# Layer 2 of a graph network: edge weights as 16-bit exponent bits, three bf16 parts of the support, and an order by hand

## The chip, the cores and the metric

The kernel runs on one core of a Trainium2 chip. The metric is the device time of one execution in microseconds (us), as the median of several executions.

Engines are named as the profile names them: PE (TensorE, matmuls), PEld (its weight loads), DVE (VectorE), ACT (ScalarE), POOL (GpSimd) and SP (which issues most transfers). PSUM is the memory in which PE leaves its sums. A record is one instruction in the profile; "issue" in a chain of waits is time in which an engine waited for nothing that the profile shows. The granted clock (PEclk) is the share of its full clock that PE ran at.

## The reference

Four graph layers act on 3327 nodes with 64 features and a dense 3327 x 3327 adjacency matrix, each as `x = x + layer(relu(layernorm(x)), adj)`. Only layer 2 is edited:

```python
def layer2(input, adj, weight, bias):
    support = input @ weight
    mask = (adj != 0).astype(support.dtype)
    rank = jnp.cumsum(mask, axis=1)
    deg = rank[:, -1:]
    k = jnp.minimum(deg, 100.0)
    pos = rank - (deg - k)
    w = mask * jnp.where(pos > 0, 0.5 ** (k - pos), 0.0)
    return w @ support + bias
```

So an edge weighs 0.5 to the power of the number of edges behind it in its row, and nothing where that is 100 or more.

## The kernel before

The nodes are 26 blocks of 128. The targets (3328 with padding) are two halves of 1664, each four quarters of 416 columns (`CH`). An accumulator bank `acc[q]` holds both halves of the aggregation: the first on PSUM partitions 0 to 63, the second on 64 to 127, because there are only 64 features. Layers 0 and 1 use the same helper.

```python
def accumulate(acc, q, h, lhsT, rhs, first, last):
    T.matmul(acc[q][h * D : (h + 1) * D, :CH], lhsT=lhsT, rhs=rhs, start=first, stop=last)
```

Layer 2 goes through the source blocks from the last. `tri` is a strict triangle with -1024 on its diagonal, `behind` the sum of the masks of all blocks already done. One number per edge slot therefore holds both the count and whether there is an edge. The weight is made of the exponent bits of a float32. In what follows, a count is a matmul with `tri` or `ones`, an accumulation one into `acc`, and a change of kind the step of PE from one to the other.

```python
for j in reversed(range(NB)):
    a = adj_block(j)                       # 128 sources x 3328 targets, f32, 3 buffers
    V.tensor_scalar(mask, a, 0.0, None, op0=OP.not_equal)
    for h in range(2):
        for q in range(NQ):
            i0 = h * HN + q * CH
            p = scratch("cnt")
            T.matmul(p[:, :CH], lhsT=tri, rhs=mask[:, i0 : i0 + CH], ...)
            if behind is not None:
                T.matmul(p[:, :CH], lhsT=ones, rhs=behind[:, i0 : i0 + CH], ...)
            S.activation(bits, p[:, :CH], AF.Relu, bias=ebias, scale=-EXP_UNIT)   # int32
            V.scalar_tensor_tensor(w, p[:, :CH], MAX_NEIGH - MASK_ON, bits.bitcast(F32),
                                   op0=OP.is_lt, op1=OP.mult)
            pending.append((q, h, m_n[:, slot(j), :], w, j == NB - 1, j == 0))
            flush(2)                       # accumulates all but the last two
    ...
    V.tensor_add(nxt, behind, mask)        # the running sum, for the next block
```

A scheduler orders the instructions of layers 0 to 2. Layer 3, the longest, is ordered by hand in both kernels.

## Time and profile before

| | before |
|---|---|
| median of the runs | 1997.71 us (1993.67 to 1998.79) |
| busy in the profiled execution (1998.0 us) | PE 68%, DVE 68%, ACT 34%, POOL 21% |
| layer 2, first count to last accumulation | 465.2 to 749.7: 284.5 us |
| one source block in it | 11.06 us |

In layer 2 the two steps from count to weight are these groups of the page. A row gives the line, engine and operation, what it writes from what and how often; then its busy time and the mean of one in ns; then the idle time of the engine ahead of it and who ended most of that.

```profile
L392 ACT ACTIVATE bits<-cnt,ebias 128x416 int32<-128x416 f32 x208 | 123.3, 607 | 167.9 <-PE cnt L384 156.0
L394 DVE SCALAR_TENSOR_TENSOR w<-cnt,bits 128x416 f32<-128x416 f32 x208 | 115.6, 586 | 50.9 <-ACT bits L392 50.7
```

They are hops from engine to engine: ACT idles mostly for the counts, DVE for ACT. Idle time of ACT here costs nothing by itself.

### The profile page before, as it was taken

The page shows a single profiled execution, that of the slowest core. Times are in us where ns is not written, and L with a number is a line of the kernel's source. Part 1 is how long each engine was busy: PE and PEld are TensorE (multiplying, and loading weights), DVE is VectorE, ACT ScalarE, POOL GpSimd, SP SyncE. Part 2 cuts the span into 40 slices and gives each one's busy share as a digit, 9 for nine tenths or more (in the row PEclk, how much of TensorE's full clock was granted, in tenths as well). Part 3 has the DMA queues.
Part 4 walks back from the last instruction along what each step waited for, and adds up shares of the span by engine and source line. Part 5 has one row for each costly group of instructions (what it writes and reads, how often), then busy time and mean ns, then how long its engine had stood idle before and what let it go on. Part 6 is the DMA issues. An engine that isn't in the chain of part 4 may idle for free.

```text
span 1998.0 us, 10423 instructions
## 1 busy us (share of the span) xinstructions
PE 1358.2 (68%) x3689; PEld 563.7 (28%) x3689; DVE 1349.5 (68%) x1269; ACT 686.8 (34%) x613; POOL 421.4 (21%) x118
## 2 busy tenths in 40 slices
PE   5999968937999992666566656646566656656640
PEld 3344333313222222222223322223223322222310
DVE  2021062067777768788888788886888788888878
ACT  0010011013444440454444445442644445444440
POOL 0000000000000000334433333440533333443330
PEclk9999988978999995666666566657665666666565
DMA  7985934961444101111111111110211111111000
GB/s 294 398 326 216 390 147 177 394 249 69 153 155 156 50 0 53 34 34 36 63 39 34 35 34 34 41 62 0 65 37 34 35 34 35 41 61 34 17 0 17
DMA packets 24373, 204.01 MB, mean 102 GB/s; under 512 B 5505, under 2 KB 5633, under 8 KB 12545
## 3 DMA queue, kind: packets, MB, share of 16 engines
q1 hardware_dynamic: 21312, 202.84, 27.1%
q10 hardware_dynamic: 3008, 0.50, 0.1%
q8 instruction: 29, 0.48, 0.1%
q14 instruction: 24, 0.19, 0.0%
HBM read 202.48 MB, written 0.85 MB: 102 GB/s over the span
## 4 chain that ended last, share of the span: by engine, by line
issue 34%; PE 27%; POOL 16%; DVE 14%; DMA 7%; ACT 1%; ACTq 0%; POOLq 0%; DVEq 0%
PE acc L233 17%; POOL lnp L567 9%; POOL sig L560 7%; DMA adj<-in_adjT 7%; DVE behind L408 2%; PE cnt L376 2%; PE cnt L384 2%; PE pd L532 1%; PE pd L535 1%; DVE sq L73 1%; PE ac L575 1%; PE pd L493 1%; DVE dist L554 1%; DVE w L394 1%; DVE den L540 1%
## 5 line engine op out<-in xcount | busy, mean ns | idle before, releaser
L532 PE MATMUL pd<-auge,augj 66*128 66x416 f32 x416 | 288.9, 791 | 237.7 <-DVE den L533 237.7
L560 POOL TENSOR_TENSOR sig<-sig,adj 128x1664 f32<-128x1664 f32 x52 | 213.1, 4117 | 1099.7 <-ACT sig L559 1099.7
L575 PE MATMUL ac<-lnp,hn 128*65 128x416 f32 x416 | 210.6, 674 | 190.2 <-DVE lnp L572 183.8
L535 PE MATMUL pd<-augd,augj 66*128 66x416 f32 x416 | 284.5, 781 | 0.0
L233 PE MATMUL acc<-adj,m_n 128*64 128x416 f32 x1056 | 270.2, 518 | 13.7 <-DMA adj<-in_adjT 13.6
L567 POOL TENSOR_TENSOR lnp<-lnp,dist 128x1664 f32<-128x1664 f32 x52 | 205.6, 3956 | 135.2 <-ACT dist L566 135.2
L544 ACT ACTIVATE den<-den 128x1664 f32<-128x1664 f32 x52 | 82.7, 1590 | 426.9 <-DVE den L540 388.5
L554 DVE TENSOR_SCALAR dist<-dist 128x1664 f32<-128x1664 f32 x52 | 222.3, 4275 | 1.8
L532 PEld LDWEIGHTS pd<-auge,augj 66*128 66x128 f32 x416 | 116.6, 288 | 361.3 <-DVE den L533 255.7
L249 DVE COPY m_t<-acc 128x416 f32<-128x416 f32 x12 | 6.3, 584 | 305.9 <-PE acc L233 305.9
L233 PE MATMUL acc<-w,m_n 128*64 128x416 f32 x416 | 184.0, 534 | 18.7 <-DVE w L394 18.7
L537 DVE SCALAR_TENSOR_TENSOR dist<-den,pd 128x416 f32<-128x416 f32 x208 | 122.4, 588 | 104.6 <-PE pd L535 95.4
L551 DVE SCALAR_TENSOR_TENSOR dist<-dist,den 128x1664 f32<-128x1664 f32 x52 | 182.0, 3501 | 9.1 <-ACT den L547 9.1
L392 ACT ACTIVATE bits<-cnt,ebias 128x416 int32<-128x416 f32 x208 | 123.3, 607 | 167.9 <-PE cnt L384 156.0
L533 DVE TENSOR_SCALAR den<-pd 128x416 f32<-128x416 f32 x208 | 122.2, 588 | 68.7 <-PE pd L532 68.3
L575 PEld LDWEIGHTS ac<-lnp,hn 128*65 128x65 f32 x416 | 72.0, 181 | 340.3 <-DVE lnp L572 216.4
L233 PEld LDWEIGHTS acc<-adj,m_n 128*64 128x64 f32 x1056 | 112.5, 136 | 168.0 <-issue 131.9
L535 PEld LDWEIGHTS pd<-augd,augj 66*128 66x128 f32 x416 | 120.8, 291 | 123.5 <-issue 103.4
L394 DVE SCALAR_TENSOR_TENSOR w<-cnt,bits 128x416 f32<-128x416 f32 x208 | 115.6, 586 | 50.9 <-ACT bits L392 50.7
L565 ACT ACTIVATE lnp<-dist,one 128x1664 f32<-128x1664 f32 x52 | 87.4, 1681 | 128.2 <-DVE dist L554 127.9
L571 DVE TENSOR_TENSOR lnp<-lnp,den 128x1664 f32<-128x1664 f32 x52 | 98.0, 1885 | 7.2 <-POOL lnp L567 7.2
L572 DVE TENSOR_TENSOR lnp<-lnp,sig 128x1664 f32<-128x1664 f32 x52 | 98.4, 1892 | 1.8
(200 smaller groups left out, 1233.0 us busy)
## 6 DMA issues: line engine op xcount, KB each, us to landing
adj<-in_adjT SPq DMA_DIRECT2D x88, 1664.0 KB, 8.4
adj<-in_adjT SPq DMA_DIRECT2D x52, 832.0 KB, 4.5
res<-in_adjT SPq DMA_DIRECT2D x4, 1664.0 KB, 8.3
xn<-in_x SPq DMA_DIRECT2D x1, 832.0 KB, 5.0
out<-u SPq DMA_DIRECT2D x1, 832.0 KB, 3.4
ih<-in_wihT ACTq DMA_DIRECT2D x4, 48.0 KB, 4.8
hh<-in_whhT ACTq DMA_DIRECT2D x4, 48.0 KB, 9.8
w<-in_W ACTq DMA_DIRECT2D x4, 16.0 KB, 5.5
```

The source lines that it names most:

```text
L233: T.matmul(acc[q][h * D : (h + 1) * D, :CH], lhsT=lhsT, rhs=rhs, start=first, stop=last)
L392: S.activation(bits, p[:, :CH], AF.Relu, bias=ebias, scale=-EXP_UNIT)
L394: V.scalar_tensor_tensor(w, p[:, :CH], MAX_NEIGH - MASK_ON, bits.bitcast(F32), op0=OP.is_lt, op1=OP.mult,)
L532: T.matmul(p[:, :CH], lhsT=lhsT, rhs=auge[:, cs], start=True, stop=True)
L533: V.tensor_scalar(e[:, cs], p[:, :CH], MIN_NORM, None, op0=OP.max)
L535: T.matmul(p[:, :CH], lhsT=lhsT, rhs=augd[:, cs], start=True, stop=True)
L537: V.scalar_tensor_tensor(d[:, cs], e[:, cs], 2e-7, p[:, :CH], op0=OP.mult, op1=OP.max)
L551: V.scalar_tensor_tensor(dist[j], dist[j], LN_SCALE**0.5, den[j], op0=OP.mult, op1=OP.mult)
L554: V.tensor_scalar(dist[j], dist[j], ONE_LESS, None, op0=OP.min)
L560: G.tensor_mul(s, s, adjs.pop((hf, j)))
L567: G.tensor_sub(l, l, dist[j])
L575: T.matmul(acc[q][: D + 1, :CH], lhsT=hn[:, slot(j), :], rhs=l[:, q * CH : (q + 1) * CH], start=j == 0, stop=j == NB - 1,)
```

## The change

The intent: take the product off DVE by letting ACT alone make the weight. With the bias changed to `(100 - 1024) * 2**7`, the ReLU gives `(100 - count) * 128` for an edge and zero otherwise. As a 16-bit integer these are the bits of a bf16 power of two, scaled by 2**-27. The support is scaled by 2**27 and cut into three bf16 parts whose sum is exact, so that all matmuls of the loop are bf16. Counts now come in tiles of two banks. A half block is one pass of the loop over `k`: two quarters of both target halves, with 8 counts and 12 accumulations. Its accumulations stand together, with the target halves alternating, and the order of the instructions is that of the text (`manual_schedule`). The rest of the diff gives up the four scratch banks of PSUM for the loop and takes them back after it (so that the two-bank count tiles fit), and removes comments.

```diff
-EXP_UNIT = 2.0**23
+EXP_UNIT = 2.0**7
...
             linear(h_t, w_l2, m_n)
+            V.tensor_scalar(m_n, m_n, 2.0**27, None, op0=OP.mult)
+            parts = []
+            for i in range(3):
+                p = mk.tile([P, NB, D], BF16, name=f"part{i}", bufs=1)
+                V.tensor_copy(p, m_n)
+                if i < 2:
+                    V.tensor_sub(m_n, m_n, p)
+                parts.append(p)
...
+            with tc.tile_pool(name="psc", bufs=2, space=PSUM) as psc, tc.manual_schedule():
...
+                def flush(keep):
+                    while len(pending) > keep:
+                        j, k, ws = pending.pop(0)
+                        for i in range(2):
+                            for n, p in enumerate(parts):
+                                for h in range(2):
+                                    accumulate(acc, 2 * k + i, h, p[:, slot(j), :],
+                                               ws[h][:, i, :].bitcast(BF16), ...)
...
+                    for k in range(NQ // 2):
+                        ws = []
+                        for h in range(2):
+                            p = psc.tile([P, 2, 512], F32, name="cnt", tag="cnt")
+                            for i in range(2):
+                                ... tri and ones matmuls into p[:, i, :CH], as before
+                            w = wk.tile([P, 2, CH], U16, name="w", tag=f"w{h}")
+                            S.activation(w, p[:, :, :CH], AF.Relu, bias=ebias, scale=-EXP_UNIT)
+                            ws.append(w)
+                        pending.append((j, k, ws))
+                        flush(1)
-                        V.scalar_tensor_tensor(w, p[:, :CH], MAX_NEIGH - MASK_ON,
-                                               bits.bitcast(F32), op0=OP.is_lt, op1=OP.mult)
```

## The prediction

Two figures in it, 176 ns and 627 ns, are estimates worked out from formulas of the pages that it names; it does not call them so. The trace has 0.18 us and 607 ns.

> **What bounds the kernel now.** I read the page's busy shares and slices first: no engine is above 68%, so the kernel is a row of stages with different limits, and the change touches one of them. The table by stages (stretches cut at the start and end of layer 2's loop) sizes it; its columns are the stretch, then busy time and instruction count of PE, PEld, DVE, ACT and POOL, the granted clock, the DMA share and GB/s.
>
> ```profile
> 415.00:465.00 50.00, 9.24 (x55) 8.02 (x54) 44.76 (x49) 6.48 (x10) 0.00 (x0) 0.59 0.33 131
> 465.00:750.00 285.00, 265.09 (x834) 68.27 (x833) 201.32 (x261) 123.31 (x208) 0.00 (x0) 1.00 0.28 102
> 800.00:1998.00 1198.00, 717.06 (x1311) 317.13 (x1309) 981.67 (x740) 529.03 (x350) 418.59 (x104) 0.61 0.11 36
> ```
>
> The reader is to see that layer 2's loop is 285 of 1998 us, that PE is busy 93% of it at full clock, and that DMA works at a quarter of its time. The other stages are not edited. Next, the chain of waits in the middle of that loop, one source block long (start, length, what):
>
> ```profile
> 559.82 1.89 DVE behind L408
> 561.72 0.51 DVE w L394
> 562.23 0.04 issue
> 562.27 0.91 PE acc L233 x2
> 563.18 0.28 PE cnt L376
> 563.47 0.18 PE cnt L384
> 563.64 0.84 PE acc L233 x2
> ...
> 570.88 1.89 DVE behind L408
> ```
>
> One block takes 570.88 - 559.82 = 11.06 us; 26 blocks make 288 us, which is the stage. 2.4 us of each block are DVE (the running sum of masks, then a weight product queued behind it) and 8.6 us are PE. Last, PE alone in order of time:
>
> ```profile
> 563.12 0.35 PE L376 MATMUL cnt<-mask,tri 128*128 128x416 bf16 x1
> 563.30 0.34 PE L384 MATMUL cnt<-behind,ones 128*128 128x416 bf16 x1
> 563.57 0.91 PE L233 MATMUL acc<-w,m_n 128*64 128x416 f32 x2
> 564.42 0.35 PE L376 MATMUL cnt<-mask,tri 128*128 128x416 bf16 x1
> 564.60 0.34 PE L384 MATMUL cnt<-behind,ones 128*128 128x416 bf16 x1
> 564.87 1.61 PE L233 MATMUL acc<-w,m_n 128*64 128x416 f32 x4
> 566.41 0.35 PE L376 MATMUL cnt<-mask,tri 128*128 128x416 bf16 x1
> ```
>
> Read starts, not lengths, because matmuls overlap. A count matmul follows another after 0.18 us. One f32 accumulation is two records (x2) and holds PE 0.85 us; two of them (x4) hold it 1.54 us, so one costs 0.70 us, plus about 0.15 us for going over to and from it. Count to accumulation is 0.27 us instead of 0.18. The unit of two counts and one accumulation repeats every 1.30 us (563.12, 564.42), and eight per block are 10.4 us: PE's own order, with 16 changes of kind per block, is nearly the whole 11.06 us.
>
> **What the Trainium skill says.** (1) "TensorEngine Tiling (Array Packing)", Key Properties: a change of the tiling mode drains TensorE, and different tiles run matmuls in parallel. Counts use all 128 columns, accumulations 64, so each change is one of mode; the trace agrees, at 0.09 us beyond the stream before and after, plus 0.05 us for the first matmul. For parallel tiles, layer 0's loop shows the two halves overlapping:
>
> ```profile
> 98.63 5.21 PE L233 MATMUL acc<-adj,m_n 128*64 128x416 f32 x19
> 104.01 12.29 PE L233 MATMUL acc<-adj,m_n 128*64 128x416 f32 x47 [0.18 <-DMA adj<-in_adjT]
> ```
>
> 47 records in 12.29 us are 0.26 us each, below the 0.35 us of one stream (0.70 / 2), though that order changes halves only every eight records. (2) "TensorE: Matmul & The Clock Gate", Back-to-back issue gap: N / 2.4 + 2.5 ns warm, 176 ns for 416 columns; the trace's 0.18 us agrees. (3) The same page, the HAM clock gate: half clock after idle; the 0.59 before the loop agrees. (4) "ScalarE: Activation LUTs", What ACT_TABLE_LOAD costs: 0.833 ns per element and about 280 ns with a pointer bias, 627 ns for 416; the trace has 607 ns.
>
> **The change, part by part, per block of sources.**
>
> Removed: eight DVE products with the weight (0.58 us each, 4.7 us). DVE keeps mask 1.88 and running sum 1.89 us, 3.8 us, and nothing in PE's way is queued behind the running sum any more. That takes the 2.4 us DVE piece off the chain.
>
> ACT: eight ACTIVATEs of 416 become four of 832. Estimate: 0.607 + 416 x 0.833 ns = 0.95 us each, 3.8 us per block, beside PE.
>
> PE, counts: the same 16 matmuls, now eight in a row twice. Eight starts: 1 x 0.186 + 6 x 0.176 + 0.27 to the first accumulation = 1.51 us. Twice: 3.0 us.
>
> PE, accumulations: each f32 one becomes three bf16 ones of 0.176 us. Alone that would be 0.53 instead of 0.70 us. But the new order alternates the halves, 64 output columns each, so I take pairs as fully parallel: twelve matmuls are six pairs, 6 x 0.176 + 0.05 + 0.09 = 1.20 us, twice 2.4 us, against 5.6 us plus changes before. This is the choice that matters most; it extends an overlap seen in f32 to bf16 and to two halves of the same PSUM bank.
>
> Sum for PE: 2 x (1.51 + 1.20) = 5.42 us per block. DVE (3.8), ACT (3.8) and DMA (1.7 MB at the 398 GB/s of layer 0 is 4.3 us, for 22 of the 26 blocks) are all below, so PE stays the bound. The listing of instruction order shows no wait against it: after the counts of one block, DVE needs 3.8 us for that sum and the next mask, and PE has about 2 x 2.7 + 1.2 = 6.6 us of work before it needs both.
>
> Added ahead of the loop, all on DVE: one scaling, three copies to bf16, two subtractions of 1664 columns. A f32 tensor_scalar of this size takes 1.02 us and a tensor_tensor 1.89 us in this trace (lines 483 and 333); copies counted like the former, 4 x 1.02 + 2 x 1.93 = 7.9 us. The listing places them after the last copy of the linear step (which ends at 466.05), ahead of the third mask; the first accumulation waits for them.
>
> Loop: parts end at 466.05 + 7.9 = 474. PE then has 26 x 2.40 = 62.4 us of accumulations and 25 x 3.02 = 75.5 us of counts (the last block's counts run beside the parts): 138 us. I add 3 us for a cold clock after that wait (estimate) and 1 us for the third mask, which needs the second block's counts first. End near 616. Before, the last accumulation ends at 749.7. The exit is some 1 us longer, as two quarters are evacuated after the end. Gain: 133 - 1 = 132 us by the bare sum. A few ns of weight load per pair (one load per 64 columns, two loads per pair, none of it seen at this pace) would add 0.01 x 6 x 52 = 3 us. I take 129 us: 1997 - 129 = **1868 us**.
>
> **Rivals.** *A: pairs don't overlap in bf16.* For it: every overlap in the trace is between different banks. Against: the records of layer 0 show that the array does it. Cost: 6 x 0.176 = 1.06 us per half block, 52 x 1.06 = 55 us, so 1923 us, still faster. *B: ACT or its PSUM buffers become the bound.* Two count tiles only, so counts for one half wait for the ACTIVATE of the half before. For it: the order listing has such a wait on each. Against: 1.9 us of ACT per half block against 2.7 us of PE. It would need an ACTIVATE of over 1.35 us; at 1.5 us it adds 0.3 x 52 = 16 us, 1884 us. *C: transfers.* At 4.3 us per block against 5.4 they have a fifth to spare; landing took a median 8.4 us, with three buffers some 16 us ahead. If each block took 6 us, 22 x 0.6 = 13 us, 1881 us. *D: the gain is given back later.* Layer 3 starts only when layer 2 is done and is not edited, so it moves forward whole. I see no mechanism for a loss.
>
> **Range and chances.** Nothing can go much below PE's bare sum, 1865 us, unless the cold start costs less; the low end is 1857. B, C, or pairs at 0.20 us each lead to 1880 to 1890; the high end is 1892. A is outside, at 5 to 7%. All leave it faster by over 2% (below 1957); I keep 2% for a stall that I overlooked.
>
> **What would show it.** Right: the loop's stretch falls from 285 to about 155 us; a block repeats every 5.4 to 5.6 us; accumulations start in pairs, 0.176 us from pair to pair; PE idles some 7 us at the start of the loop for the parts; DVE is near 70% busy in it; stages before and after keep their lengths within 2 us. Wrong: accumulations starting singly every 0.176 us (A); PE waiting for ACT at each count (B); the mask waiting for DMA (C); a layer 3 longer than before (D).

## The result, and the profile after

The changed kernel took 1859.16 us (median of 4, 1857.56 to 1864.29) against 1997.71 us. The ratio is 0.9314, with a 95% interval of 0.9298 to 0.933. Here and below, a ratio is the mean time of one kernel's fast runs over that of the kernel before in the same rounds, so it is not quite the ratio of the medians.

The table by stages of the changed kernel, with cuts at the same places of the program (columns as in the prediction):

```profile
468.00:620.00 152.00, 143.13 (x1044) 68.71 (x1042) 100.32 (x62) 93.61 (x104) 0.00 (x0) 0.98 0.54 198
665.00:1856.70 1191.70, 714.53 (x1309) 315.56 (x1307) 980.55 (x738) 529.04 (x350) 418.42 (x104) 0.61 0.11 36
```

The loop fell from 285 to 152 us at these cuts; from first count to last accumulation it is 467.6 to 615.7, 148.1 us. PE is still busy 94% of it, DVE 66%. The chain of waits in the middle of the loop, for one half block:

```profile
540.69 1.18 PE acc L240 x12
541.87 0.28 PE cnt L409
542.15 0.18 PE cnt L417
...
543.03 0.18 PE cnt L409
543.20 0.18 PE cnt L417
543.38 1.18 PE acc L240 x12
```

Only PE is left on the chain. The twelve accumulations (x12) take 1.18 us, and a half block 543.38 - 540.69 = 2.69 us. Start by start, the trace has pairs 3 to 4 ns apart and 0.176 us from pair to pair (0.197 after the first). The weight's single step is now

```profile
L425 ACT ACTIVATE w<-cnt,ebias 128x832 uint16<-128x832 f32 x104 | 93.6, 950 | 62.8 <-PE cnt L417 52.7
```

The start of the loop, PE in order of time:

```profile
470.47 0.37 PE L240 MATMUL acc<-w,part 128*64 128x416 bf16 x2
472.75 0.37 PE L240 MATMUL acc<-w,part 128*64 128x416 bf16 x2 [1.91 <-DVE part L372]
475.73 1.60 PE L240 MATMUL acc<-w,part 128*64 128x416 bf16 x8 [2.62 <-DVE part L372]
```

The first two accumulations run as soon as the first part is made; then PE idles 1.91 and 2.62 us for the second and third part. After that it runs at half pace until 481.9, with counts 0.35 us apart. This start has a part in the experiments.

### The profile page after: what moved, and what is told of

Same layout as the page of the kernel before. It is cut to its first block, busy times and chain, and to the rows that moved or that the text cites. A ratio compares the mean times of both kernels' runs of the same rounds, so it can differ in the third digit from the quotient of the medians.

```text
span 1856.7 us, 10430 instructions
## 1 busy us (share of the span) xinstructions
PE 1231.3 (66%) x3897; PEld 561.0 (30%) x3897; DVE 1245.1 (67%) x1067; ACT 657.1 (35%) x509; POOL 421.2 (23%) x118
## 4 chain that ended last, share of the span: by engine, by line
PE 30%; issue 26%; DVE 24%; POOL 11%; DMA 8%; ACT 1%; ACTq 0%; POOLq 0%; DVEq 0%
PE acc L240 13%; DMA adj<-in_adjT 7%; POOL lnp L595 6%; POOL sig L588 5%; PE pd L560 5%; PE pd L563 5%; DVE dist L582 5%; DVE dist L579 4%; PE cnt L409 2%; DVE lnp L600 2%; DVE lnp L599 2%; PE cnt L417 2%; DVE den L568 1%; DVE sq L74 1%; PE ac L603 1%
## 5 line engine op out<-in xcount | busy, mean ns | idle before, releaser
L425 ACT ACTIVATE w<-cnt,ebias 128x832 uint16<-128x832 f32 x104 | 93.6, 950 | 62.8 <-PE cnt L417 52.7
L568 DVE TENSOR_TENSOR den<-den,dist 128x1664 f32<-128x1664 f32 x52 | 98.4, 1891 | 1.8
L279 ACT ACTIVATE gate<-gate,brz 128x416 f32<-128x416 f32 x16 | 9.7, 606 | 235.2 <-PE gate L277 235.2
```

## The experiments

Each kernel is the changed kernel with one edit, unless it says otherwise. Loop times are from the profiled execution, from first count to last accumulation. Medians of all runs are in the table; the kernel before was run beside each, at medians of 1997.05 to 1997.61 us.

| run | edit | median us | ratio to before (95%) | loop us | us per block |
|---|---|---|---|---|---|
| before | | 1997.71 | 1 | 284.5 | 11.06 |
| changed | | 1859.16 | 0.9314 (0.9298, 0.9330) | 148.1 | 5.38 |
| one_column | no overlap of halves (wrong result) | 1912.93 | 0.9574 (0.9558, 0.9590) | 198.5 | 7.48 |
| halves_in_turn | six of one half, six of the other | 1879.26 | 0.9405 (0.9391, 0.9419) | 165.6 | 6.13 |
| f32_weights | f32 instead of bf16 parts | 1872.63 | 0.9373 (0.9359, 0.9387) | 159.2 | 6.12 |
| before_paired | kernel before, halves paired | 1908.73 | 0.9550 (0.9534, 0.9566) | 198.8 | 7.65 |
| product_back | product on DVE again | 2024.62 | 1.0134 (1.0112, 1.0156) | 318.5 | 12.3 |
| product_masks_first | the same, masks ahead of it | 1947.97 | 0.9752 (0.9736, 0.9767) | 231.8 | 8.8 |
| by_scheduler | no order by hand | 1854.51 | 0.9278 (0.9261, 0.9295) | 140.6 | 5.38 |
| start_hidden | start mended, first try | 1868.98 | 0.9355 (0.9331, 0.9380) | 141.2 | 5.38 |
| start_hidden2 | start mended | 1855.66 | 0.9285 (0.9270, 0.9301) | 141.2 | 5.38 |
| two_parts | two bf16 parts | 1837.83 | 0.9198 (0.9179, 0.9218) | 127.7 | 4.67 |
| two_by_scheduler | two parts, no order by hand | 1845.06 | 0.9239 (0.9224, 0.9254) | 132.5 | 4.67 to 5.85 |
| two_hidden2 | two parts, start mended | 1833.74 | 0.9182 (0.9166, 0.9198) | 123.6 | 4.67 |

### Do the halves overlap? one_column and halves_in_turn

My theory was that the alternating halves run in pairs on the two halves of the PE array. The rival was that the gain comes from bf16 and from fewer changes of kind alone.

```diff
-    accumulate(acc, 2 * k + i, h, ...)
+    accumulate(acc, 2 * k + i, h if j == NB - 1 else 0, ...)   # one_column: wrong on purpose
```

> Wrong result on purpose: after the first block, the second half's accumulations go to the first half's 64 columns, so no two of them can overlap. My theory (the alternating halves run in pairs on the two halves of the PE array, 0.176 us per pair) expects six matmuls more in the row per half block: 6 x 0.176 x 50 = 53 us more, about 1912 us, half-block period 3.7 us instead of 2.69. Rival (accumulations do not overlap; the gain is all from fewer changes of kind and from bf16): no change, 1859 us.

Measured: 1912.93 us, with the result wrong (relative error 0.36). PE in order of time:

```profile
541.79 2.30 PE L240 MATMUL acc<-w,part 128*64 128x416 bf16 x12
544.02 0.35 PE L409 MATMUL cnt<-mask,tri 128*128 128x416 bf16 x1
```

The twelve accumulations hold PE for 544.02 - 541.79 = 2.23 us instead of 1.18. The loop is 50 us longer. The overlap is shown, also for two halves of one bank.

```diff
-    for i in range(2):
-        for n, p in enumerate(parts):
-            for h in range(2):
+    for h in range(2):                    # halves_in_turn
+        for i in range(2):
+            for n, p in enumerate(parts):
```

> Same instructions, but six accumulations of one half and then six of the other. Theory with a look-ahead of about four matmuls (in layer 0 of the kernel before, the second half's stream starts with the fifth record of the first half's eight): the second half starts with the third of the first, so 8 steps instead of 6: 2 x 0.176 x 52 = 18 us more, 1877 us. If the order did not matter: 1859 us. If nothing overlapped unless strictly alternating: 1912 us.

Measured: 1879.26 us, and per group:

```profile
542.26 1.62 PE L240 MATMUL acc<-w,part 128*64 128x416 bf16 x12
543.82 0.35 PE L409 MATMUL cnt<-mask,tri 128*128 128x416 bf16 x1
```

That is 1.56 us, 0.38 more than alternating, which is two steps of 0.176. The records show the second half's first matmul at 542.646, 6 ns after the first half's third at 542.640, with three of the first half then still to start. (The records do not name the half; their starts fall into two streams, each with 0.20 us to its second matmul and 0.176 from there on.) The text of the kernel, which `manual_schedule` keeps, has six and then six. So PE does not start these matmuls in program order, but it looks ahead only a few for work for the idle half; the alternation is worth 17 us of the loop.

### What are the bf16 parts worth? f32_weights and two_parts

```diff
-EXP_UNIT = 2.0**7
+EXP_UNIT = 2.0**23
-    (three parts)
+    parts = [m_n]
-    w = wk.tile([P, 2, CH], U16, ...)
+    w = wk.tile([P, 2, CH], I32, ...)     # read as F32 by the matmul
```

> Order, tiles and pairs of the changed kernel, but f32: 32-bit exponent bits from ACT, the f32 support, no parts. Theory (the three bf16 parts are worth only 0.70 against 0.53 us per accumulation, paired): half block 2.69 -> 3.06 us, 52 x 0.35 = 18 us more in the loop, 6 us less at its start (no parts): 1870 us. Rival (bf16 is the main source of the gain): over 1930 us.

Measured: 1872.63 us. A half block is 3.06 us instead of 2.69, as expected, and the loop is 11 us longer. The bf16 parts, which name the change, are worth some 13 us of 139; the pairs, the missing product and the order carry the rest. What the wider count tiles are worth alone was not tested.

In two_parts, `range(3)` becomes `range(2)`:

> Two bf16 parts of the support instead of three (16 bits of it are kept, so the result is less exact). Theory: two pairs less per half block, 52 x 2 x 0.176 = 18 us, and 2.9 us less DVE work ahead of the loop: 1838 us, half-block period 2.34 us. Rival (ACT or the two count tiles are nearly the bound): ACT's 1.9 us still fits, but a chain count - ACT - count above 2.34 us would leave over 1845 us.

Measured: 1837.83 us and 2.34 us per half block. So ACT and the two count tiles still leave room at that pace. The run passed the comparison with the reference; how much larger its error is was not reported.

### Does the product on DVE matter? before_paired, product_back and product_masks_first

before_paired is the kernel before, with the loops over `q` and `h` exchanged and two accumulations flushed at a time:

```diff
-    for h in range(2):
-        for q in range(NQ):
+    for q in range(NQ):
+        for h in range(2):
             ...
-            flush(2)
+        flush(2)
```

> The kernel before with one change: the two halves of a quarter are counted one after the other and their two f32 accumulations follow one another, so that they can pair and the changes of kind fall from 359 to 205. Theory: PE 4 x 1.65 = 6.6 us per block, so DVE with 8 products of 0.51 and 3.85 us of masks and sums, 8.0 us or a little more with its waits, becomes the bound: 26 x 2.8 = 70 us less, about 1925 us (to 1945). Rival (the order without the ACT part gives the whole gain): 1870 us. Rival (nothing without bf16): 1997 us.

Measured: 1908.73 us, better than I expected. In its loop DVE is busy 185.76 of 190 us:

```profile
470.00:660.00 190.00, 188.46 (x794) 58.91 (x790) 185.76 (x246) 110.30 (x200) 0.00 (x0) 1.00 0.43 153
```

DVE has become the bound, at 7.65 us per block; my 8.0 had the products and masks slightly too long. PE's records cover the loop too, but its accumulation pairs alternate between 0.85 us and about 1.35, where the second half waits for its product. So a large part of the gain was to be had in f32 by the order alone, and the product stops it there.

The other way round, product_back adds to the changed kernel one product on DVE per tile, in place on the bits:

```diff
     S.activation(w, p[:, :, :CH], AF.Relu, bias=ebias, scale=-EXP_UNIT)
+    V.scalar_tensor_tensor(w.bitcast(BF16), p[:, :, :CH], MAX_NEIGH - MASK_ON,
+                           w.bitcast(BF16), op0=OP.is_lt, op1=OP.mult)
```

> The changed kernel with the product on DVE put back (four per block, 832 columns, in place on the ACT's bits). Theory: DVE then has 3.8 + 4 x about 1.0 = 7.8 us per block, more than PE's 5.38, and becomes the bound: 26 x 2.5 = 65 us more, about 1924 us, PE waiting for DVE. Rival (PE's order alone made the gain, DVE had room): under 1870 us.

Measured: 2024.62 us, 100 more than expected and 1.3% above the kernel before, clear of noise. DVE is busy only 180 of 290 us in the loop, so its load is not the bound. The chain of waits shows what is:

```profile
601.78 0.96 ACT w L425
602.75 0.03 issue
602.77 1.96 DVE w L428 x2
604.73 1.80 DVE behind L443
606.53 1.81 DVE mask L402
608.34 0.05 issue
608.39 0.53 PE cnt L409
```

DVE takes its queue in order. The running sum and the next mask stand behind the block's last two products, which wait for ACT, which waits for the counts; the next counts wait for the mask. PE idles about 4.7 us per block and falls to half clock again and again (its granted clock is 0.78 on average over those 290 us). To test that reading, product_masks_first emits the running sum and the next mask ahead of the products and changes nothing else:

```diff
+    nxt = ...; V.tensor_add(nxt, behind, mask)   # before the counts of this block
+    ahead = make_mask(j - 1)
     for k in range(NQ // 2):
         ... counts, ACT, product, accumulations
-    V.tensor_add(nxt, behind, mask)
```

> The kernel with the DVE product put back took 2025 us where I had expected 1924: in its trace the next block's mask and the running sum stand behind the four products in DVE's queue, and PE waits 4.7 us per block for the mask. Here DVE does the running sum and the next mask ahead of the four products; nothing else differs. Theory (order of DVE's queue): PE's wait for the mask goes. What is left is DVE's 3.75 us of masks and some 5 to 6 us for the four products, which hold the two count tiles in turn (count 0.9, ACT 0.95, DVE 1.02): 8.8 to 9.7 us per block instead of 12.3, so 1940 to 1965 us. Rival (two count tiles held by DVE set the pace, whatever the order): 2000 us or more. If DVE's busy time alone counted: 7.7 us per block, 1920 us.

Measured: 1947.97 us, inside the expected range. The order of DVE's queue made 77 us of the loss of 165. In what is left, the chain of waits has

```profile
569.01 1.02 DVE w L438
570.04 1.80 DVE behind L410
571.84 1.80 DVE mask L401
573.64 0.94 DVE w L438
574.58 0.04 issue
574.62 0.34 PE cnt L419
```

The counts now wait for products, which hold the two count tiles, and some products wait for the running sum and the mask. DVE makes up 80% of this chain, ACT and the counts the rest. DVE is busy 177 of 210 us in the loop, so its load alone is not the bound here either. A third count tile was not tried.

### The order by hand, and the start of the loop

```diff
-    with tc.tile_pool(name="psc", bufs=2, space=PSUM) as psc, tc.manual_schedule():
+    with tc.tile_pool(name="psc", bufs=2, space=PSUM) as psc:      # by_scheduler
```

> The changed kernel without the order by hand. The instruction listing shows 107 changes of kind instead of 101, and some pairs torn apart in the first blocks. Theory: the order in the text is nearly what the scheduler takes too, so within 5 us of 1859 us. Rival (the order by hand is worth much): over 1880 us.

Measured: 1854.51 us, as expected within 5 us, but on the fast side, with a loop 7.5 us shorter. The steady blocks are the same 5.38 us. The start differs:

```profile
472.88 0.54 PE L240 MATMUL acc<-w,part 128*64 128x416 bf16 x2
473.35 0.35 PE L409 MATMUL cnt<-mask,tri 128*128 128x416 bf16 x1
473.54 0.34 PE L417 MATMUL cnt<-mask,ones 128*128 128x416 bf16 x1
```

The scheduler put the second block's counts among the first block's accumulations. PE works on them while DVE makes the parts, and its granted clock stays at 1.00 from 469 to 486. With three parts the order by hand is thus no part of the gain; it costs some 5 us. I tried the same by hand:

```diff
-    flush(1)
+    flush(1 if j < NB - 2 else 3)          # counts of two blocks before the first accumulation
-    V.tensor_scalar(m_n, m_n, 2.0**27, ...)
+    V.tensor_scalar(w_l2, w_l2, 2.0**27, ...)   # start_hidden: on the weights, once
     # and: the parts of the odd slots first, those of the even ones later, between masks
```

> Three parts as in the changed kernel, but the start is mended: 2**27 folded into the weights, the parts of the odd slots first and of the even ones later between masks, and the counts of two blocks ahead of the first accumulation. Theory: of the 8.1 us from the first count to the end of the parts, PE idles 4.5 us and is cold for some 2.7 us after; about 5 us of it go: 1854 us. If the loop end is set elsewhere: 1859 us.

Measured: 1868.98 us, a miss. The loop did shrink to 141.2 us, but it began 16 us later. The view of DVE in order of time shows why, at the very start of the program:

```profile
38.52 0.23 DVE L185 TENSOR_SCALAR w_l<-w_l 128x128 f32<-128x128 f32 x1 [15.51 <-DMA w_l<-in_L2w]
```

The small scaling had been placed early in DVE's queue and stood there 15.51 us for its weights, with layer 0 behind it. In start_hidden2 the factor sits in the copies out of PSUM after the linear step:

> As start_hidden, whose loop was 7 us shorter but whose first count came 16 us later, because the scaling of the weights stood in DVE's queue at the program's start and waited 15.5 us for their transfer. Here the factor 2**27 is in the copies out of PSUM after the linear step, at no added instruction. Theory: first count near 468 us as in the changed kernel, loop about 141 us, 1852 us. If something else delayed that kernel: still over 1860 us.

Measured: 1855.66 us (1850.69 to 1858.43), with the first count at 470.0. The delay is gone and the loop is 141.2 us. Its interval against the kernel before (0.9270 to 0.9301) overlaps a little with that of the changed kernel, so a whole-run gain is likely but not clear.

Both mended starts were also run with two parts.

> start_hidden2 with two parts instead of three. Theory: both gains add, but the parts that are hidden are now fewer: loop 127.7 us (two parts alone) less about 5 us: 1832 us. If PE's start is set by the counts alone: 1838 us.

> Two parts, order left to the scheduler. By scheduler the three-part loop took 140.6 instead of 148.1 us, since the listing has counts of the second block among the first accumulations. Theory: the same hiding with two parts, loop about 122 us, 1832 us. If the scheduler needs the third part's time to order well: 1838 us.

Measured: 1833.74 and 1845.06 us. The first has the lowest median, though its interval overlaps that of two_parts (0.9166 to 0.9198 against 0.9179 to 0.9218); it beats both kernels, at the price of a support kept to 16 bits. The second fell short of 1832 and of its rival's 1838: in seven of its 26 blocks the scheduler tore the accumulations apart. The chain of waits of one such block has

```profile
547.39 0.96 ACT w L425
548.35 0.04 issue
548.39 0.34 PE cnt L409
```

Here all counts of the block stand almost together, and the third group of them must wait until ACT has emptied one of the two count tiles: in the records a count starts 0.74 us after the one before it instead of 0.18. Later an accumulation is 0.27 us late behind another ACTIVATE, and one that stands alone among the counts costs two more changes of kind. Such blocks take 5.85 us instead of 4.67. That more count tiles would cure it is likely, but was not run. With two parts, the order by hand is worth some 7 us (1845.06 - 1837.83, two_parts), and 11 with the mended start (1845.06 - 1833.74).

## Why the prediction was right

- **The bound and the block.** Right. PE's own order set most of the pace before (8.6 of 11.06 us per block) and sets it after: 2.69 us per half block against 1.51 + 1.20 = 2.71. One count was off without effect: the kernel before has 14 changes of kind per block (359 in all), not 16, since two of the eight accumulations follow each other. The overlap of the halves, the choice that mattered most, is shown by one_column: rival A was predicted at 55 us and cost 54 (1912.93 - 1859.16).
- **The product off DVE.** Right in direction, and more needed than I wrote: product_back lost all of the gain. What matters is less the 4.7 us than that nothing waits ahead of the masks.
- **Rivals B and C.** Neither came. ACT took 0.950 us per tile (estimate 0.95) and was busy 66% of the steady loop; DMA worked 61% of it. B exists all the same: it shows in two_by_scheduler, where the order lets the counts run into it.
- **The start.** The work was right, the wait was not. The scaling, copies and subtractions took 1.03 and 1.89 us each, as counted, and the parts were done at 475.7 (474 predicted). But the first accumulation did not wait for all of them: PE idled 1.91 + 2.62 = 4.5 us, where the prediction's sign was 7. The cold clock cost about 2.7 us (3 assumed), and PE waited 0.64 us for the third mask (1 assumed).
- **The size.** The gain was 139 us, and I had taken 129. Two terms make most of the difference. The 3 us for weight loads per pair were not needed: pairs came every 0.176 us. And the stretch after the loop was 1240.9 us instead of 1248.2, though it is not edited: the sign that the stages around the loop keep their lengths within 2 us failed. (The first count also came 2.4 us later, at 467.6 instead of 465.2.) Its steady groups have the same period of 43.6 us in both traces. The 7 us lie in the stretches ahead of, between and after its two passes, where PE transposes. In the first, PE's transposes took 12.4 instead of 14.6 us, under a granted clock of 0.89 instead of 0.62. Over all 14 profiles this stretch ranges from 1240.8 to 1248.2 us, and the two highest (1248.2 and 1246.8) belong to the kernel before and before_paired. But start_hidden2, of the new form, has 1245.4. Whether this is chance of the clock's phase, or follows in part from the older form, stays open. These 7 us are luck as far as the prediction goes: without them the changed kernel would stand near 1866, next to the predicted 1868.

A ladder of runs sorts the gain: 1997.7 us before; 1908.7 with the halves paired (before_paired); 1872.6 with the product gone and the accumulations grouped (f32_weights); 1859.2 with bf16. The step to f32_weights also brings the wider count tiles and the order by hand; no run takes it apart further.

## What to carry to other kernels

Where matmuls fill only half of the PE columns, put those of the two halves directly next to one another: here that turned twelve matmuls from 2.23 into 1.18 us, and it did more than the smaller data type (54 us against 13). Take an elementwise step off a queue in which later blocks' inputs stand, or emit those inputs first; an engine at 62% busy can still hold up everything. And look at the start of a loop separately: a wait there or one misplaced small instruction cost 7 to 16 us.

## What the Trainium skill lacked or had wrong

- "TensorEngine Tiling (Array Packing)", Key Properties, says that a change of tiling mode drains TensorE but not what it costs. Here a count followed by an accumulation takes 0.27 us instead of 0.18, and the way back 0.27 instead of 0.18: 0.09 us each way.
- "TensorE: Matmul & The Clock Gate", Back-to-back issue gap, gives a sustained 131 ns for N = 512 and says that N / 2.4 + 2.5 over-counts at large N. For N = 416 the runs show 176 ns in every steady bf16 stream at full clock, which is the formula.
- The same page's Part 3 says that matmuls start in program order, without reordering. In halves_in_turn, whose program has six accumulations of one column half and then six of the other, the second half started 6 ns after the third of the first half's six. No page says how far this look-ahead goes.
- Part 3 measures column packing for 32 columns; for two halves of 64 in one PSUM bank, the runs show a factor of 2.23 / 1.18 = 1.9.
